# A two-layer graph attention kernel on one core: rows loaded one unit ahead, softmax work moved, bias rows prepared in pass one

## The chip, the core and the metric

The kernel runs on one core of a Trainium2 chip. Five engines work side by side: TensorE (PE; its weight loads are listed as PEld), VectorE (DVE), ScalarE (ACT), GpSimd (POOL) and SyncE (SP), which here issues every DMA. Each engine takes its instructions in the order of the program, and an instruction waits until what it reads has been written and what it overwrites has been read. Times are device microseconds (us); the metric is the time of one execution.

## What is computed

The input x has 128 batch entries of 64 rows by 768 columns, adj one 64 by 64 mask per entry. With `h = relu(layernorm(x))`, two layers follow:

```
m_left, m_right = h @ W_left.T, h @ W_right.T
u = h @ m_left.T / temper            (upper triangle and diagonal of adj)
  + h @ m_right.T / temper           (lower triangle)
e = exp(u) * adj
attention = e / (sum(e, axis=2) + 1e-10)
ctx = attention @ (h @ W_lin.T + b_lin)
h = relu(layernorm(ctx) * ln_a + ln_b)
```

The result is x plus the h of the second layer. Everything is float32.

## The kernel before, in words

The batch is cut into 16 units of 512 rows (T = 512, NB = 16). Each layer makes two passes over the units. **Pass one** projects a unit with W_left (k = 0) and W_right (k = 1) and makes its attention; **pass two** makes h @ W_lin, the context and the layer norm. In layer 0 pass two leaves its rows in DRAM, and pass one of layer 1 reads them back.

`project(u, k, g)` (lines 291 to 325) makes a third of one projection as seven groups of matmuls (a Strassen-like scheme, table ORDER at line 121). A unit has 42 such groups. Four PSUM banks, X, Y, Z and V, each with one buffer, take the groups in the order X Y Z V X Z V. ACT empties X (lines 312 and 320), DVE empties Y, Z and V (lines 315, 318, 322), and a bank is written again two or three groups later. So PE stops soon after DVE or ACT stops. The sums of token halves, T1 to T4 (line 140), are made on POOL; group Y reads T2, the first Z reads T1, the first V T3 and the last V T4. `scores(u)` (line 327) runs on PE between the second and third group of unit u + 1.

All other work of a pass is cut into steps that wait in a list, `queue`. After each group `pump(1)` (line 325) puts one step into the program; `flush()` puts all that are left. Where a step stands in the list thus sets where its instructions stand on every engine. For the next unit the steps are, in the order of the list before:

- the softmax chain of the unit just scored, in six steps (lines 341 to 365), with its eight stores of `att`;
- in layer 0, the statistics and the scaling of the new rows (lines 211 to 228); then four block transposes (line 257) and `store`, four DMAs to DRAM (line 250);
- `load_h` (line 191), which reads the transposed unit back as `ht`, four empty steps, and in layer 1 six `affine` steps, ScalarE's scaling and relu of `ht` (line 198);
- the four sums T1 to T4 and the masks `wm` (line 281).

The DMAs that load the rows and the masks `adj` of unit u + 1 are issued by `load` (line 269) in unit u after its first project, behind the stores of `att`. In the second unit (u = 1) of each pass one, `one_aside` also loads W_lin, centres it (`centre`, line 96) and makes its sums on POOL. Pass two begins with the load of the bias rows b1 and b2 and the arithmetic on them (lines 420 to 428). In the last unit of pass two of layer 0, rows of layer 1's first unit are loaded, transposed and scaled (lines 560 and 561).

Of the kernel before, what the change touches and what calls it, by code (L numbers as in the profile page):

```python
# [10 lines left out]
F32 = mybir.dt.float32  # L11
I32 = mybir.dt.int32
AF = mybir.ActivationFunctionType
# [4 lines left out]
def kernel(  # L18
# [60 lines left out]
    def flush(keep=0):  # L79
        pump(len(queue) - keep)  # L80
# [99 lines left out]
    def load_rows(l, u, pool):  # L180

        XR[l, u] = []
        for g in range(2):
            t = pool.tile([P, 2, H], F32, name="x", bufs=2)
            for a in range(4):
                i = 4 * g + a
                src = x[u * NBB + i] if l == 0 else ROWS[u][i]
                nc.sync.dma_start(t[a * 32:(a + 1) * 32], src.rearrange("(k j) h -> j k h", k=2))
            XR[l, u].extend([t[:, 0, :], t[:, 1, :]])

    def load_h(which, l, u):
        ht = HT[which, l, u] = big.tile([P, C, T], F32, name="ht")
        nc.sync.dma_start(ht, KEPT[l][u])

    def affine(which, l, u):

        for c in range(C if l else 0):
            queue.append(lambda c=c: nc.scalar.activation(  # L198
                HT[which, l, u][:, c, :], HT[which, l, u][:, c, :], AF.Relu,
                bias=b_col[:, c:c + 1], scale=a_col[:, c:c + 1]))  # L200

    def transpose_rows(l, u, pool):

# [41 lines left out]
            queue.append(lambda: nc.sync.dma_start(KEPT[l][u], ht))  # L245
            return

        xb = pool.tile([P, H // 32, Q, 32], F32, name="n" if pool is big else "xb", bufs=2 if pool is big else 1)

        def store():  # L250
            to = KEPT[l][u].rearrange("(b i) c t -> i c b t", b=4)
# [5 lines left out]
            queue.append(lambda q=q: nc.vector.transpose(  # L257
                xb[:, :, q, :], xr[q].rearrange("p (b j) -> p b j", j=32)))
        queue.append(store)
        queue.append(lambda: load_h(1, l, u))  # L260
        queue.extend([lambda: None] * 4)
        affine(1, l, u)


    def pass_one(l, aside):
        with tc.tile_pool(name=f"one{l}", bufs=2, reuse_waits="tile") as sp:
            ADJ, WM = {}, {}

            def load(u):
                if (l, u) not in XR:  # L270
                    load_rows(l, u, sp)
# [55 lines left out]
            def scores(u):  # L327
# [36 lines left out]
                        for g in range(2):  # L364
                            nc.sync.dma_start(to[a // 2, a % 2, g], at[a * 32:(a + 1) * 32, g])  # L365

                it = chain()
                for _ in range(6):
                    queue.append(lambda: next(it, None))

            for u in range(NB):
                if u == 0:
                    load(0)
                    if l == 0:
                        load_w(0, "l")
                        prepare(0, nc.vector)

                        flush(keep=5)
                        tokens = [queue.popleft() for _ in range(5)]
                        sums_w(0, "l", nc.vector)  # L380
                        sums = [queue.popleft() for _ in range(4)]
                        queue.extend(sums[:2] + tokens[:2] + [sums[2], tokens[2], sums[3], tokens[3], tokens[4]])
                        load_w(0, "r")
                        sums_w(0, "r", nc.gpsimd)
                    else:
                        prepare(0)
                    flush()
                    load(1)
                for g in range(CH):
                    project(u, 0, g, (lambda: scores(u - 1)) if u and g == 0 else None)  # L390
                    if g == 0:
                        if u and u + 1 < NB:
                            load(u + 1)
                        if u + 1 < NB:
                            prepare(u + 1)
                        else:
                            load_h(2, l, 0)
                            queue.extend([lambda: None] * 4)
                            affine(2, l, 0)
                            sums_t((2, l, 0))  # L400
                        if u in aside:
                            aside[u]()
                for g in range(CH):
                    project(u, 1, g)
                flush()
            scores(NB - 1)
            flush()


    def pass_two(l, aside):  # L410
        last = l == L - 1
        with tc.tile_pool(name=f"two{l}", bufs=2, reuse_waits="tile") as sp:
            rows = {}

            def row(name, src, n0=0, n1=H):
                t = sp.tile([P, n1 - n0], F32, name=name, bufs=1)
                nc.sync.dma_start(t, bass.AP(tensor=src.tensor, offset=src.offset + n0, ap=[[0, P], [1, n1 - n0]]))
                rows[name] = t

            row("b1", b_lin[l], 0, HH)  # L420
            row("b2", b_lin[l], HH, H)
            bm = stat.tile([P, 2], F32, name="bm", bufs=1)
            nc.vector.reduce_sum(bm[:, 0:1], rows["b1"], axis=mybir.AxisListType.X)
            nc.vector.reduce_sum(bm[:, 1:2], rows["b2"], axis=mybir.AxisListType.X)
            nc.vector.tensor_add(bm[:, 0:1], bm[:, 0:1], bm[:, 1:2])
            nc.vector.tensor_scalar_mul(bm[:, 0:1], bm[:, 0:1], -1.0 / H)
            nc.gpsimd.tensor_sub(rows["b2"], rows["b2"], rows["b1"])
            nc.vector.tensor_scalar_add(rows["b1"], rows["b1"], bm[:, 0:1])
            if last:
                row("a", ln_a[l])  # L430
                row("b", ln_b[l])
            AT, HL = {}, {}

            def load(u):
# [21 lines left out]

            def finish(u, r):
                cx = context(u, r)
                zs = [sp.tile([P, H], F32, name="z", bufs=2 if last else 4) for _ in range(2)]
                xs = []  # L460
                if last:
                    for k in range(2):
# [83 lines left out]
            for u in range(NB):  # L546
                for r in range(2):
                    before = None
                    if u or r:
                        before = lambda: finish(*((u, 0) if r else (u - 1, 1)))  # L550
                    kept = list(queue)
                    queue.clear()
                    beside = deque()
                    nxt = (2, l, u + 1) if u + 1 < NB else None if last else (1, 1, 0)
                    if r == 0:
                        if u + 1 < NB:
                            load(u + 1)
                            affine(*nxt)
# [3 lines left out]
                        if u + 1 < NB:  # L562
                            queue.extendleft([lambda: None] * (7 - len(queue)))
                        if u in aside:
                            loaded = aside[u]()
                    else:
                        if nxt:
                            sums_t(nxt)
# [57 lines left out]
```

## Time and profile before

| | |
|---|---|
| median of three runs | 3449.06 us (3445.66 to 3449.86) |
| profiled execution, its own time | 3446.99 us |
| its span, first to last instruction | 3445.2 us |
| PE busy | 3020.3 us, 88% of the span |
| POOL / DVE / ACT busy | 770.7 / 1142.9 / 586.5 us |
| mean granted TensorE clock | 0.937 of full speed |

The busy times are totals over passes with different limits. The granted clock is either 1.0 or 0.5 in a stretch (2.4 or 1.2 GHz), so a mean below 1 tells what share of the time it stood at the lower level. Of a wait the profile gives the engine that waited, the instruction that ended the wait, and the line of each.

### The profile page before, as it was taken

What the parts mean: (1) busy time and instruction counts of PE and PEld (TensorE: products, weight loads), DVE (VectorE), ACT (ScalarE), POOL (GpSimd) and SP (SyncE); (2) the same over time, 40 slices, a digit from 0 to 9 for tenths busy, and PEclk for the clock granted to TensorE, in tenths of its full rate; (3) what the DMA queues carried; (4) which work ended last, traced back from release to release, by engine and by line L of the source; (5) the groups of instructions that cost most, each with busy time, mean ns of one, the idle gap of its engine ahead of it and who ended that gap; (6) DMA issues with size and microseconds to landing.
All of it is one profiled execution on the core that took longest, in us unless ns stands there. A gap on an engine that the chain in (4) does not pass through costs nothing. (4 is left out here: it accounts for less than half of the span.)

```text
span 3445.2 us, 37340 instructions
## 1 busy us (share of the span) xinstructions
PE 3020.3 (88%) x14872; PEld 2310.3 (67%) x14872; DVE 1142.9 (33%) x2310; ACT 586.5 (17%) x1114; POOL 770.7 (22%) x484
## 2 busy tenths in 40 slices
PE   7888888888888899999787888877887789999998
PEld 6777777777777655555576777766776678555554
DVE  4433333333333232223232222222222222466555
ACT  2111111111111122222211111111111111222221
POOL 2210011000110253232103100000000111455554
PEclk9998999989999999999898999998898889999999
DMA  5323322223222243333432222223232220455554
GB/s 153 88 71 72 78 79 60 73 70 78 78 60 78 72 148 103 106 115 113 116 88 60 60 60 60 61 63 77 64 74 70 71 60 21 141 159 147 165 165 125
DMA packets 228718, 310.22 MB, mean 90 GB/s; under 512 B 53696, under 2 KB 179136, under 8 KB 220352
## 3 DMA queue, kind: packets, MB, share of 16 engines
q1 hardware_dynamic: 228544, 307.84, 32.8%
q8 instruction: 117, 1.92, 0.2%
q14 instruction: 57, 0.47, 0.0%
HBM read 202.91 MB, written 104.86 MB: 89 GB/s over the span
## 5 line engine op out<-in xcount | busy, mean ns | idle before, releaser
L140 POOL TENSOR_TENSOR ts<-ht 128x768 f32<-128x768 f32 x126 | 243.5, 1933 | 2069.6 <-ACT ht L198 850.3
L301 PE MATMUL Z<-ht,w_l_S 128*128 128x256 f32 x576 | 182.6, 464 | 250.5 <-DVE u L318 250.5
L301 PE MATMUL X<-ht,w_r_A 128*128 128x256 f32 x1152 | 302.0, 401 | 111.8 <-ACT n L320 111.8
L301 PEld LDWEIGHTS X<-ht,w_r_A 128*128 128x128 f32 x1152 | 229.5, 201 | 150.6 <-ACT n L320 117.8
L301 PEld LDWEIGHTS Z<-ht,w_l_S 128*128 128x128 f32 x576 | 130.0, 232 | 283.0 <-DVE u L318 262.1
L301 PE MATMUL V<-ts,w_l_A 128*128 128x256 f32 x1152 | 306.0, 406 | 0.3 <-DVE n L322 0.3
L516 PE MATMUL X<-w_n_A,ht 128*128 128x384 f32 x768 | 273.0, 492 | 17.7 <-DVE s L521 17.7
L301 PE MATMUL X<-ht,w_l_A 128*128 128x256 f32 x1152 | 281.0, 380 | 2.5 <-ACT s L312 2.5
L301 PE MATMUL V<-ts,w_r_A 128*128 128x256 f32 x1152 | 280.0, 379 | 0.0
L516 PE MATMUL V<-w_n_A,ts 128*128 128x384 f32 x768 | 268.8, 486 | 0.0
L301 PEld LDWEIGHTS V<-ts,w_l_A 128*128 128x128 f32 x1152 | 239.7, 208 | 40.5 <-DVE n L322 1.7
L315 DVE TENSOR_TENSOR u<-Y,s 128x256 f32<-128x256 f32 x192 | 80.3, 418 | 507.8 <-PE Y L301 454.8
L322 DVE TENSOR_TENSOR n<-V,u 128x256 f32<-128x256 f32 x384 | 161.6, 421 | 255.4 <-PE V L301 251.5
L140 POOL TENSOR_TENSOR ts<-ht,ts 128x768 f32<-128x768 f32 x126 | 238.8, 1895 | 26.4 <-issue 24.5
L301 PEld LDWEIGHTS X<-ht,w_l_A 128*128 128x128 f32 x1152 | 220.7, 192 | 34.8 <-ACT s L312 3.3
L301 PEld LDWEIGHTS V<-ts,w_r_A 128*128 128x128 f32 x1152 | 218.9, 190 | 29.8
L516 PEld LDWEIGHTS X<-w_n_A,ht 128*128 128x128 f32 x768 | 147.2, 192 | 121.4 <-DVE s L521 19.0
L516 PEld LDWEIGHTS V<-w_n_A,ts 128*128 128x128 f32 x768 | 146.2, 190 | 102.2 <-issue 0.8
L472 ACT ACTIVATE z<-aux 128x768 f32<-128x768 f32 x128 | 102.5, 806 | 622.5 <-PE aux L450 622.4
L198 ACT ACTIVATE ht<-ht,b_col,a_col 128x512 f32<-128x512 f32 x192 | 142.2, 804 | 328.0 <-DMA ht<-h 328.0
L312 ACT COPY s<-X 128x256 f32<-128x256 f32 x192 | 71.4, 372 | 738.9 <-PE X L301 732.8
L320 ACT COPY n<-X 128x256 f32<-128x256 f32 x192 | 71.1, 370 | 701.0 <-PE X L301 700.8
(102 smaller groups left out, 3864.0 us busy)
## 6 DMA issues: line engine op xcount, KB each, us to landing
ht<-h SPq DMA_DIRECT2D x63, 1536.0 KB, 6.5
h<-xb SPq DMA_DIRECT2D x120, 384.0 KB, 6.0
x<-in_x_dram SPq DMA_DIRECT2D x128, 192.0 KB, 4.8
z<-z SPq DMA_DIRECT2D x128, 192.0 KB, 2.9
x<-z SPq DMA_DIRECT2D x128, 192.0 KB, 4.7
xr<-in_x_dram SPq DMA_DIRECT2D x128, 192.0 KB, 4.0
out_dram<-xr SPq DMA_DIRECT2D x128, 192.0 KB, 2.7
adj<-in_adj_dram SPq DMA_DIRECT2D x64, 128.0 KB, 6.0
```

What stands on the lines that cost most here:

```text
L140: eng.tensor_sub(b[o], b[m], b[n])
L198: queue.append(lambda c=c: nc.scalar.activation(HT[which, l, u][:, c, :], HT[which, l, u][:, c, :], AF.Relu, bias=b_col[:, c:c + 1], scale ...
L301: nc.tensor.matmul(p, w[a][:, c, g * P:(g + 1) * P], b[t][:, c, :], start=(new and c == 0), stop=(c == CH - 1), skip_group_check=True)
L312: nc.scalar.copy(s1, p)
L315: nc.vector.tensor_add(u2, p, s1)
L320: nc.scalar.copy(to, pb)
L322: nc.vector.tensor_add(to, pb, (u4 if i == 3 else u2).rearrange("p (b s) -> p b s", s=S))
L472: nc.scalar.activation(zs[k].rearrange(two, n=2), cx[k], AF.Square, accum_out=ss[:, k:k + 1])
L516: nc.tensor.matmul(p, b[t][:, c, r * P:(r + 1) * P], w[a][:, c, :], start=(new and c == 0), stop=(c == CH - 1), skip_group_check=True)
```

## The change

- `load_rows` for unit u + 2 is now a step of unit u, behind `load_h` of unit u + 1; before, the rows of unit u + 1 were loaded in unit u. The steps of a unit begin with the first project, not with the second, so the statistics or transposes come first.
- The six softmax steps stand behind `load_h` and `load_rows`; then come `load_adj`, six empty steps, the six affine steps in layer 1, masks, T1 and T2. T3 and T4 (`late`) are put in during the last project of the unit.
- In the last unit the next pass's `load_h` and its affine steps and sums take these places.
- The bias rows are loaded, and worked on as one more step, in unit 1 of pass one (`bias`, called from `one_aside`).
- At the end of pass two of layer 0, layer 1's first rows are loaded in unit 14, transposed in its second half, and read back and scaled in unit 15. Affine steps of pass two go in pairs, those of layer 1's first unit in threes; z has two buffers where it had four in layer 0.

The core of the diff (the new `affine` with a step, and `row`, moved out of pass two, are left out):

```diff
@@ transpose_rows
         queue.append(store)
-        queue.append(lambda: load_h(1, l, u))
-        queue.extend([lambda: None] * 4)
-        affine(1, l, u)
@@ pass_one
-            def prepare(u, eng=nc.gpsimd):
-                if (1, l, u) not in TS:
-                    transpose_rows(l, u, sp)
-                    sums_t((1, l, u), eng)
-                queue.append(lambda: masks(u))
+            def softmax(u):
+                return [lambda: next(CHAIN[u], None)] * 6
+            def prepare(u):
+                transpose_rows(l, u, sp)
+                queue.append(lambda: load_h(1, l, u))
+                if u + 1 < NB:
+                    queue.append(lambda: load_rows(l, u + 1, sp))
+                queue.extend(softmax(u - 2) if u > 1 else [lambda: None] * 6)
+                queue.append(lambda: load_adj(u))
+                queue.extend([lambda: None] * 6)
+                affine(1, l, u)
+                queue.append(lambda: masks(u))
+                sums_t((1, l, u))
...
-                it = chain()
-                for _ in range(6):
-                    queue.append(lambda: next(it, None))
+                CHAIN[u] = chain()
...
+            load_rows(l, 1, sp)
             for u in range(NB):
                 if u == 0:
+                    queue.extend([lambda: None] * 7)
+                if u + 1 < NB:
+                    prepare(u + 1)
+                else:
+                    queue.extend([lambda: None] * 6)
+                    queue.append(lambda: load_h(2, l, 0))
+                    queue.extend(softmax(u - 1) + [lambda: None] * 4)
+                    affine(2, l, 0)
+                    sums_t((2, l, 0))
+                late = [queue.pop() for _ in range(2)][::-1]
+                for k in range(2):
+                    for g in range(CH):
+                        project(u, k, g, (lambda: scores(u - 1)) if u and k == g == 0 else None)
+                        if k == g == 0 and u in aside:
                             aside[u]()
-                for g in range(CH):
-                    project(u, 1, g)
+                        if k == 1 and g == CH - 2:
+                            flush()
+                            queue.extend([lambda: None] * 3 + late)
                 flush()
...
+    def bias(l):
+        row("b1", b_lin[l], 0, HH, big)
+        row("b2", b_lin[l], HH, H, big)
+        b1, b2 = rows["b1"], rows["b2"]
+        bm = stat.tile([P, 2], F32, name="bm", bufs=1)
+        def centred():
+            nc.vector.reduce_sum(bm[:, 0:1], b1, axis=mybir.AxisListType.X)
+            nc.vector.reduce_sum(bm[:, 1:2], b2, axis=mybir.AxisListType.X)
+            nc.vector.tensor_add(bm[:, 0:1], bm[:, 0:1], bm[:, 1:2])
+            nc.vector.tensor_scalar_mul(bm[:, 0:1], bm[:, 0:1], -1.0 / H)
+            nc.gpsimd.tensor_sub(b2, b2, b1)
+            nc.vector.tensor_scalar_add(b1, b1, bm[:, 0:1])
+        queue.append(centred)
@@ pass_two
-                        elif nxt:
-                            load_rows(1, 0, sp)
-                            transpose_rows(1, 0, big)
+                            if turn:
+                                load_rows(1, 0, sp)
+                        elif turn:
+                            queue.append(lambda: load_h(1, 1, 0))
+                            queue.extend(nop * 4)
+                            affine(1, 1, 0, 3)
@@ one_aside
             load_w(l, "n")
+            bias(l)
             centre(l)
```

On PE the order of the work is unchanged. Three places show the new order.

The SP queue in a steady unit of layer 0's pass one (`h_8` is the transposed unit 8, `att_6` the attention of unit 6, `x` rows), before:

```order
L365 DMA att_6_131<-at 128x1x32 x8
L188 DMA x<-in_x_dram 32x2x768 x8
L274 DMA adj<-in_adj_dram 64x4x128 x2
L253 DMA h_8_85<-xb 192x4x128 x4
L193 DMA ht<-h_8_85 128x3072
```

and now:

```order
L256 DMA h_8_85<-xb 192x4x128 x4
L193 DMA ht<-h_8_85 128x3072
L188 DMA x<-in_x_dram 32x2x768 x8
L373 DMA att_6_131<-at 128x1x32 x8
L272 DMA adj<-in_adj_dram 64x4x128 x2
```

The rows x were those that the four stores of h_8 wait for; now they are those of unit 9. The masks `adj` came ahead of the store and are now the last of the turn.

DVE where the statistics of new rows begin in layer 0 (Y, Z and V rows empty banks, the first of them in the unit's second group), before:

```order
L355 RECIPROCAL s<-s 128x4
L356 TENSOR_TENSOR v<-v,s 128x256
L322 TENSOR_TENSOR n<-V,u_961 128x4x64
L360 STREAM_TRANSPOSE at<-v 128x4x2x32
L174 BN_STATS st<-x 128x6 x2
L175 BN_AGGR mv_1071<-st 128x2
L315 TENSOR_TENSOR u_1090<-Y,s_1080 128x256
L174 BN_STATS st<-x 128x6 x2
L175 BN_AGGR mv_1071<-st 128x2
L318 TENSOR_TENSOR u_1100<-Z,u_1090 128x256
```

and now:

```order
L330 TENSOR_TENSOR n<-V,u_943 128x4x64
L174 BN_STATS st<-x 128x6 x2
L175 BN_AGGR mv_972<-st 128x2
L323 TENSOR_TENSOR u_991<-Y,s_981 128x256
L174 BN_STATS st<-x 128x6 x2
L175 BN_AGGR mv_972<-st 128x2
L326 TENSOR_TENSOR u_1052<-Z,u_991 128x256
```

The statistics follow the last V of the unit before; the softmax rows stand behind the transposes.

POOL in unit 1 of layer 0 (`ts` are T1 to T4, `wm` the masks, `w_n` is W_lin, `b` the bias rows), before:

```order
L140 TENSOR_TENSOR ts<-ht 128x768
L140 TENSOR_TENSOR ts<-ht,ts 128x768
L140 TENSOR_TENSOR ts<-ht 128x768
L140 TENSOR_TENSOR ts<-ht,ts 128x768
L281 TENSOR_TENSOR wm<-adj,tri 128x4x64 x2
L110 TENSOR_TENSOR w_n_A_703<-w_n_A_703,wm 128x1152
```

and now:

```order
L279 TENSOR_TENSOR wm<-adj,tri 128x4x64 x2
L140 TENSOR_TENSOR ts<-ht 128x768
L140 TENSOR_TENSOR ts<-ht,ts 128x768
L439 TENSOR_TENSOR b_713<-b_713,b_711 128x384
L110 TENSOR_TENSOR w_n_A_700<-w_n_A_700,wm 128x1152
L110 TENSOR_TENSOR w_n_A_701<-w_n_A_701,wm 128x1152
L110 TENSOR_TENSOR w_n_A_703<-w_n_A_703,wm 128x1152
L110 TENSOR_TENSOR w_n_A_702<-w_n_A_702,wm 128x1152
L118 TENSOR_TENSOR w_n_S_704<-w_n_A_701,w_n_A_702 128x1152
L118 TENSOR_TENSOR w_n_S_705<-w_n_S_704,w_n_A_700 128x1152
L118 TENSOR_TENSOR w_n_A_701<-w_n_A_700,w_n_A_701 128x1152
L118 TENSOR_TENSOR w_n_S_706<-w_n_A_703,w_n_S_705 128x1152
```

The masks now precede the sums, and T3 and T4 of this unit (the next two L140 rows in the queue) stand behind all the work on W_lin; in every other unit they follow T2 directly.

## Rows read from the trace of the kernel before

**Rows 1.** Each pass: us; busy us (instructions) of PE, PEld, DVE, ACT, POOL; PEclk; DMA.

```profile
22.70:1158.30 1135.60, 1000.66 (x5570) 872.84 (x5568) 385.95 (x884) 177.23 (x313) 164.79 (x106) 0.93 0.29 75
1158.30:1668.20 509.90, 491.66 (x1858) 271.49 (x1856) 145.24 (x303) 119.97 (x225) 166.77 (x105) 0.98 0.38 118
1668.20:2930.30 1262.10, 1030.24 (x5572) 889.69 (x5569) 306.81 (x670) 150.19 (x311) 156.06 (x104) 0.90 0.26 65
2930.30:3445.20 514.90, 492.11 (x1858) 271.57 (x1856) 295.24 (x429) 130.41 (x252) 280.60 (x157) 0.98 0.53 151
```

**Rows 2.** What PE waited for, whole span: total us, times, longest.

```profile
PE Z L301 <- DVE u L318: 251.4, 30, 11.5
PE X L301 <- ACT n L320: 111.8, 15, 8.9
PE X L516 <- DVE s L521: 17.7, 2, 9.1
```

**Rows 3.** Timeline (start us, us, engine, line, xcount) of PE without a stall, end of layer 0's pass one.

```profile
1103.63 1.46 PE L301 MATMUL X<-ht,w_l_A 128*128 128x256 f32 x6
...
1152.94 5.46 PE L335 MATMUL aux<-n,ht 128*64 128x128 f32 x96
1158.33 2.20 PE L516 MATMUL X<-w_n_A,ht 128*128 128x384 f32 x6
```

**Rows 4.** Timeline of a stall in layer 0; [idle before, and what ended it].

```profile
397.29 3.82 SPq L188 DMA_DIRECT2D x<-in_x_dram  x8
...
403.30 1.02 DVE L174 BATCH_NORM_STATS2 st<-x 128x6 f32<-128x384 f32 x2 [11.20 <-DMA x<-in_x_dram]
...
406.43 2.93 PE L301 MATMUL Z<-ht,w_l_S 128*128 128x256 f32 x6 [8.66 <-DVE u L318]
...
409.16 2.61 PE L301 MATMUL V<-ts,w_l_A 128*128 128x256 f32 x6
...
420.91 5.21 SPq L253 DMA_DIRECT2D h<-xb  x4
```

**Rows 5.** Timeline of layer 1's second stall: store, load back, affine.

```profile
2253.95 5.21 SPq L253 DMA_DIRECT2D h<-xb  x4
...
2264.43 0.34 SPq L193 DMA_DIRECT2D ht<-h  x1
...
2271.35 0.81 ACT L198 ACTIVATE ht<-ht,b_col,a_col 128x512 f32<-128x512 f32 x1 [14.02 <-DMA ht<-h]
```

**Rows 6.** Timeline around the stalls of layer 0's pass two: first unit, last unit.

```profile
1174.35 0.42 DVE L428 TENSOR_SCALAR b<-b,bm 128x384 f32<-128x384 f32 x1 [1.07 <-POOL b L427]
...
1650.86 4.33 ACT L198 ACTIVATE ht<-ht,b_col,a_col 128x512 f32<-128x512 f32 x6 [19.17 <-DMA ht<-h]
...
1659.73 4.21 PE L516 MATMUL Z<-w_n_S,ht 128*128 128x384 f32 x6 [9.09 <-DVE u L529]
```

**Rows 7.** Groups by line: xcount | busy us, mean ns | idle before.

```profile
L140 POOL TENSOR_TENSOR ts<-ht 128x768 f32<-128x768 f32 x126 | 243.5, 1933 | 2069.6 <-ACT ht L198 850.3 <-DMA ht<-h 735.6 <-PE Y L301 292.8
L281 POOL TENSOR_TENSOR wm<-adj,tri 128x256 f32<-128x256 f32 x64 | 45.1, 726 | 24.9 <-DMA adj<-in_adj_dram 24.9
L110 POOL TENSOR_TENSOR w_n_A<-w_n_A,wm 128x1152 f32<-128x1152 f32 x8 | 16.6, 2114 | 0.0
L118 POOL TENSOR_TENSOR w_n_S<-w_n_A,w_n_A 128x1152 f32<-128x1152 f32 x2 | 5.3, 2626 | 0.2
L103 DVE TENSOR_REDUCE wm<-w_n_A 128x3 f32<-128x1152 f32 x4 | 5.4, 1341 | 0.0
```

**Rows 8.** DMA issues: KB each, median us from issue to landing.

```profile
ht<-h SPq DMA_DIRECT2D x63, 1536.0 KB, 6.5
x<-z SPq DMA_DIRECT2D x128, 192.0 KB, 4.7
w_n_A<-in_w_lin_dram SPq DMA_DIRECT2D x8, 576.0 KB, 7.7
adj<-in_adj_dram SPq DMA_DIRECT2D x64, 128.0 KB, 6.0
```

More of the change, by code (lines that the diff above doesn't have):

```diff
@@ L193, in load_h, with affine, part @@
         nc.sync.dma_start(ht, KEPT[l][u])
[L195 to L200, printed above, removed]
+    def affine(which, l, u, step=1):
+        def part(c0):
+            for c in range(c0, c0 + step):
+                ht = HT[which, l, u][:, c, :]
+                nc.scalar.activation(ht, ht, AF.Relu, bias=b_col[:, c:c + 1], scale=a_col[:, c:c + 1])
+        for c in range(0, C if l else 0, step):
+            queue.append(lambda c=c: part(c))
     def transpose_rows(l, u, pool):
@@ L246, in transpose_rows @@
             return
-        xb = pool.tile([P, H // 32, Q, 32], F32, name="n" if pool is big else "xb", bufs=2 if pool is big else 1)
+        xb = pool.tile([P, H // 32, Q, 32], F32, name="xb", bufs=1)
         def store():
@@ L259, in transpose_rows, with load_adj @@
         queue.append(store)
-        queue.append(lambda: load_h(1, l, u))
-        queue.extend([lambda: None] * 4)
-        affine(1, l, u)
     def pass_one(l, aside):
         with tc.tile_pool(name=f"one{l}", bufs=2, reuse_waits="tile") as sp:
[L267 to L271, printed above, removed]
+            ADJ, WM, CHAIN = {}, {}, {}
+            def load_adj(u):
                 ADJ[u] = sp.tile([P, Q, 2, S], F32, name="adj")
@@ L365, in chain @@
                             nc.sync.dma_start(to[a // 2, a % 2, g], at[a * 32:(a + 1) * 32, g])
-                it = chain()
-                for _ in range(6):
-                    queue.append(lambda: next(it, None))
+                CHAIN[u] = chain()
+            if (l, 0) not in XR:
+                load_rows(l, 0, sp)
+            load_adj(0)
+            if l == 0:
+                load_w(0, "l")
+                transpose_rows(0, 0, sp)
+                flush()
+                sums_t((1, 0, 0), nc.vector)
+                tokens = [queue.popleft() for _ in range(4)]
+                sums_w(0, "l", nc.vector)
+                sums = [queue.popleft() for _ in range(4)]
+                queue.extend(sums[:2] + tokens[:2] + [sums[2], tokens[2], sums[3], tokens[3]])
+                load_w(0, "r")
+                sums_w(0, "r", nc.gpsimd)
@@ L371, in pass_one @@
+            queue.append(lambda: masks(0))
+            flush()
+            load_rows(l, 1, sp)
             for u in range(NB):
                 if u == 0:
[L373 to L386, printed above, removed]
@@ L387, in pass_one @@
-                    flush()
-                    load(1)
-                for g in range(CH):
[L390 to L401, printed above, removed]
+                    queue.extend([lambda: None] * 7)
@@ L402, in pass_one, with row @@
                             aside[u]()
-                for g in range(CH):
-                    project(u, 1, g)
+                        if k == 1 and g == CH - 2:
+                            flush()
+                            queue.extend([lambda: None] * 3 + late)
                 flush()
             scores(NB - 1)
+            queue.extend(softmax(NB - 1))
             flush()
+    rows = {}
+    def row(name, src, n0, n1, pool):
+        t = rows[name] = pool.tile([P, n1 - n0], F32, name=name, bufs=1)
+        nc.sync.dma_start(t, bass.AP(tensor=src.tensor, offset=src.offset + n0, ap=[[0, P], [1, n1 - n0]]))
@@ L412, in pass_two @@
         with tc.tile_pool(name=f"two{l}", bufs=2, reuse_waits="tile") as sp:
[L413 to L428, printed above, removed]
             if last:
-                row("a", ln_a[l])
-                row("b", ln_b[l])
+                row("a", ln_a[l], 0, H, sp)
+                row("b", ln_b[l], 0, H, sp)
             AT, HL = {}, {}
@@ L458, in finish @@
                 cx = context(u, r)
-                zs = [sp.tile([P, H], F32, name="z", bufs=2 if last else 4) for _ in range(2)]
+                zs = [sp.tile([P, H], F32, name="z", bufs=2) for _ in range(2)]
                 xs = []
@@ L553, in pass_two @@
                     beside = deque()
-                    nxt = (2, l, u + 1) if u + 1 < NB else None if last else (1, 1, 0)
+                    nop = [lambda: None]
+                    turn = not last and u >= NB - 2
                     if r == 0:
@@ L557, in pass_two @@
                             load(u + 1)
-                            affine(*nxt)
-                        elif nxt:
-                            load_rows(1, 0, sp)
-                            transpose_rows(1, 0, big)
-                        if u + 1 < NB:
-                            queue.extendleft([lambda: None] * (7 - len(queue)))
+                            queue.extend(nop * 3)
+                            affine(2, l, u + 1, 2)
+                            if turn:
[4 more added lines that the diff above has]
+                            affine(1, 1, 0, 3)
+                        queue.extend(nop * (7 - len(queue)))
                         if u in aside:
@@ L566, in pass_two @@
                     else:
-                        if nxt:
-                            sums_t(nxt)
+                        if u + 1 < NB:
+                            sums_t((2, l, u + 1))
+                            if turn:
+                                transpose_rows(1, 0, sp)
+                        elif turn:
+                            sums_t((1, 1, 0))
                         if u in aside:
```

## The prediction
> **What bounds the kernel now.** Read the passes first [rows 1]. Both passes two are nearly full: PE is busy for 491.7 of 509.9 us and 492.1 of 514.9, at a granted clock of 0.98. The loss is in the passes one, 1135.6 and 1262.1 us for the same work, at 0.93 and 0.90. Next, what PE waits for [rows 2]: 30 waits end with DVE's line 318 (251.4 us), 15 with ACT's line 320 (111.8 us). Both lines only empty banks, in under half a microsecond; they are late because something ahead of them on their engine is. The timelines say what. In layer 0 DVE stands at the statistics of new rows until the rows land, 11.2 us, and PE behind it for 8.66 [rows 4]. In layer 1 DVE stands at the transposes in the same way, and a second time ACT stands 14.0 us at the first affine step, whose `ht` was asked for only 6.9 us earlier [rows 5].
>
> How long would a pass one be without stalls? In [rows 3] no row has idle time before it: from 1103.63 to 1152.94 are 38 groups, 1.298 us each, and the scores take 5.4 (to 1158.33). A unit is 42 x 1.298 + 5.4 = 59.9 us, sixteen are 958. Against [rows 1], stalls cost 1135.6 - 958 = 177 us in layer 0 and 1262.1 - 958 = 304 in layer 1. That is more than PE's idle time, since after a stall two groups run at the lower clock: 2.93 and 2.61 us where 1.46 is usual [rows 4], some 2.6 us per stall.
>
> **The change part by part.** I give places in a unit as us from its start; group n ends at 1.3 n, and 5.4 later from the third on.
>
> *Layer 0, statistics.* The rows of unit u + 2 are now issued in unit u behind `load_h`, some 35 us before they are used; one such set needs 397.29 to 403.30, 6 us, before DVE can start [rows 4]. The wait goes in all units but unit 0: there the seven empty steps keep the statistics where they stood, and its rows are loaded where they were. I leave one stall, 8.4 (251.4/30) + 2.6, about 10. Gain 177 - 10 = 167.
>
> *Layer 1.* The transposes gain in the same way. The affine steps: the store now comes at about 12 (two transposes must follow the banks emptied behind the scores). From store to the first affine took 17.4 us (2253.95 to 2271.35) [rows 5], so `ht` is there at 29.4. The first affine stands behind group 21, at 5.4 + 27.3 = 32.7; PE would stop only if the X of group 22 were not copied by the second X, at 37.9. The cover is 3 us to ACT and about 7 to PE. It would shrink if the rows, 8 x 192 KB issued just behind `ht`, shared its transfer: at most doubled, 6.5 us more [rows 8], which uses up that cover and no more. Gain 304.
>
> *Bias, turn of the layers.* The stalls at the start of both passes two (17.7 us together [rows 2]) and in the last unit of layer 0's pass two (9.09, behind six affine steps in one piece [rows 6]) have their cause moved away. With some 2.4 us each of slow groups (4.21 where 2.10 is usual [rows 6]) that is 27 + 7 = 34.
>
> *What becomes late next: the masks.* In layer 0, statistics to store took 403.30 to 420.91, 17.6 us [rows 4]; begun at 0.5, with the scores between, the store comes at 23.5. `load_h` waits 10.5 for its landing [rows 5] (34), lands 7 later (41), the rows behind it need another 7 (48), the eight `att` stores about 1.5, then `adj` 3 to 6 [rows 8]: 53 to 55.5. POOL then makes two halves of the masks (1.45) and T1 and T2 (1.93 each [rows 7]), done at 58.3 to 60.8. The next unit's second group needs T2 at 61.2. T3 and T4 follow by 64.7, needed from 69.2. I take no stall, with 0.4 to 3 us of cover. The softmax steps (DVE, ACT) fall where nothing waits; their `att` stores are inside this turn.
>
> *Unit 1 with W_lin.* Here the added work is not free. DVE's update of b1 must wait for POOL's subtraction, which reads b1 and stands behind masks, T1 and T2. In layer 0 DVE gets there at about 49 and POOL at 58 + 1.0: ten microseconds in which no bank is emptied. Then come two rounds of reductions (2 x 1.34 and small ones each [rows 7]). PE loses about 12 with its slow groups. POOL's four subtractions (2.1 each) and four sums (2.6 each [rows 7]) now stand ahead of T3 and T4, 19 us; T3 comes some 3 us late, 6 with slow groups: 18 in all. In layer 1 the weights are issued behind the rows (4 x 576 KB, about 11 us at the rate of `ht`), `adj` behind them, so POOL is as late, and DVE reaches b1 at 46: 13 us of block, 15 lost, 1 more for T3: 16. For the two units I take 34, with ends 0 (POOL early, DVE never blocked) and 60 (the block twice as long).
>
> *Small ends:* where passes change, memory taken over from the last `att` stores, and ACT between affine and squares: 4, ends 0 and 10.
>
> **Sum.** 167 + 304 + 34 - 34 - 4 = 467. From the span of 3445.2 that leaves 2978; this execution's own time lies 1.8 us above its span, so **2980 us**. The execution's 3446.99 stands 2 us below the median of the runs, 3449.06, within their scatter. About 0.2%, 7 us, is what a measurement of this kernel tells from no change.
>
> **Rivals.**
>
> *Late masks.* The turn of SP grows by a few us more, and PE waits at each unit's second group in layer 0 (line 140 ends the wait). Against: 0.4 to 3 us of cover with each transfer set behind the last. For: that cover is thin, and 8 small stores are between. A miss of 2 to 5 us in 14 units is 28 to 70: 3008 to 3050. Chance 0.12.
>
> *Late `ht` in layer 1.* If rows and `ht` share the transfer and the rest slips too, ACT stands at the affine as now. One stall of 111.8/15 = 7.5 [rows 2] + 2.6 in 14 units is 141: about 3121. Against: the 7 us of cover. Chance 0.05.
>
> *The clock does not come back.* PE's waits sum to some 394 us (380.9 in [rows 2] and 13 in single ones), the stalls to about 515 (177 + 304 + 34): 121 us are slow groups. If short waits for banks kept the clock dropping even so, about 110 of them stay: 3090. Against: both passes two hold 0.98 with the same four banks [rows 1], and the groups of [rows 3] are all at full speed. The Trainium skill ("TensorE: Matmul & The Clock Gate", A second HAM failure mode: psum-queue depth-cycling) states that cycling through PSUM banks can make PE idle so often and briefly that its clock swings between the levels; by that page this rival would be the forecast, and no stretch here without a long stall shows it. Chance 0.04.
>
> *The early load does nothing.* If the rows are still behind in SP's queue when DVE asks, layer 0 keeps its 167 and the forecast is 3147. Against: the 35 us. Chance 0.02.
>
> *Slower: SP's turn longer than a unit.* A unit now takes 75 us on average, (1135.6 + 1262.1)/32 [rows 1]. Everything of the next unit hangs on `adj` at the end of SP's turn. If each of its 23 DMAs waited for the landing of the last, the turn would be about 23 x 4 to 6 us behind the store at 23.5, 115 and more: 40 us over today's unit, some 28 x 40 = 1100 above 3447, about 4500. It decides from the point where `adj` lands beyond 70, 15 later than worked out. Against: today's eight row loads are issued in 3.82 us, none waiting for another [rows 4]. Chance 0.02.
>
> **How the numbers follow.** The forecast has 0.75. Its own range: 34 can be 0 to 60, the small ends 0 to 10, unit 0's stall 6 to 11, which gives 2940 to 3012; all ends at zero together is unlikely, so I start at 2950. Taking in late masks up to 3050 leaves out the other rivals, 0.13, and the edges. Range 2950 to 3050. Faster by over 0.2%: 0.97, all cases but the last, less 0.01 for a mixture of several that ends within 0.2%; slower: 0.02.
>
> **What would show it.** The list of PE's waits should lose nearly all of lines 318 and 320 (in the old numbering): from 45 to some 5. Pass one should take about 980 us in both layers, at a granted clock near 1.0. What remains should stand in units 0 and 1 of layer 0 and in unit 1 of layer 1, ended by DVE behind the bias update (waiting for POOL), and by POOL's T3 in unit 2. Waits ended by line 140 at the second group of every unit of layer 0 would show late masks; waits of X on ACT in layer 1 a late `ht`; full busy at a clock below 0.97 the clock. A pass one above 1020 us in either layer makes the forecast wrong.

## The result and the profile after

| | before | after |
|---|---|---|
| median | 3449.46 us (4 runs, 3445.66 to 3450.26) | 2994.46 us (4 runs, 2993.47 to 2995.75) |
| ratio | | 0.8683, 95% interval 0.8668 to 0.8698 |
| span of the profiled execution | 3445.2 us | 2994.0 us |
| PE busy | 3020.3 us, 88% | 2919.1 us, 97% |
| mean granted clock | 0.937 | 0.992 |

Forecast: 2980 us, 2950 to 3050, faster. The time lies 14 us above the forecast and inside the range.

The passes of the kernel after, in the columns of [rows 1]:

```profile
21.80:1011.70 989.90, 968.46 (x5570) 852.30 (x5569) 381.51 (x889) 173.54 (x312) 166.58 (x109) 0.99 0.33 87
1011.70:1503.60 491.90, 489.01 (x1859) 270.38 (x1857) 143.10 (x298) 120.18 (x226) 165.86 (x104) 1.00 0.39 122
1503.60:2477.70 974.10, 962.60 (x5569) 848.85 (x5568) 307.75 (x675) 150.79 (x311) 156.75 (x105) 0.99 0.33 85
2477.70:2994.00 516.30, 493.81 (x1858) 272.15 (x1856) 294.31 (x424) 130.30 (x252) 279.60 (x156) 0.99 0.53 150
```

The passes one lost 145.7 and 288.0 us, the first pass two 18.0. The last pass two, 514.9 before, is no shorter. DVE, ACT and POOL did the same work as before; only its place changed.

What PE waits for, in the columns of [rows 2]. Line 326 was line 318, 328 was 320, 535 was 516, and 548 was 529:

```profile
PE Z L309 <- DVE u L326: 17.5, 4, 8.9
PE aux L240 <- DMA adj<-in_adj_dram: 12.2, 1, 12.2
PE Z L535 <- DVE u L548: 7.9, 2, 5.0
PE Z L309 <- DVE n L330: 6.9, 1, 6.9
...
PE V L309 <- POOL ts L140: 3.7, 2, 3.4
PE Y L309 <- POOL ts L140: 2.6, 1, 2.6
```

The 30 waits on line 318 are 4, the 15 on ACT's line 320 are gone, and so are the two at the bias rows (17.7 us). The 12.2 us are the start of the kernel.

A steady unit of layer 0, in the columns of [rows 3, 4]:

```profile
346.46 1.46 PE L309 MATMUL X<-ht,w_l_A 128*128 128x256 f32 x6
...
370.42 5.48 SPq L256 DMA_DIRECT2D h<-xb  x4
381.00 0.35 SPq L193 DMA_DIRECT2D ht<-h  x1
381.44 6.91 SPq L188 DMA_DIRECT2D x<-in_x_dram  x8
389.05 6.62 SPq L373 DMA_DIRECT2D att<-at  x8
395.71 1.30 SPq L272 DMA_DIRECT2D adj<-in_adj_dram  x2
399.39 1.41 POOL L279 TENSOR_TENSOR wm<-adj,tri 128x256 f32<-128x256 f32 x2 [51.17 <-DMA adj<-in_adj_dram]
...
402.65 1.81 POOL L140 TENSOR_TENSOR ts<-ht,ts 128x768 f32<-128x768 f32 x1
...
407.73 1.46 PE L309 MATMUL Y<-ts,w_l_S 128*128 128x256 f32 x6
```

The unit begins at 346.46 with its first X. The store is issued 24.0 us later, `load_h` 34.5, the masks' load 49.3, and T2 is done at 402.65 + 1.81 = 404.46, or 58.0. The next unit's Y, which reads T2, starts at 407.73 without a wait: 3.3 us of cover. In the steady units nothing on DVE waits for rows any more. From one start of the scores to the next lie 60.0 us in each of the units 3 to 14, in both layers (forecast: 59.9).

### The profile page after: what moved, and what is told of

It is laid out like the page before. It is cut to its first block, busy times and chain, and to the rows that moved or that the text cites. A ratio compares the mean times of both kernels' runs of the same rounds, so it can differ in the third digit from the quotient of the medians.

```text
span 2994.0 us, 37473 instructions
## 1 busy us (share of the span) xinstructions
PE 2919.1 (97%) x14872; PEld 2248.1 (75%) x14872; DVE 1135.8 (38%) x2310; ACT 583.2 (19%) x1112; POOL 769.9 (26%) x484
## 4 chain that ended last, share of the span: by engine, by line
PE 89%; DMA 4%; POOL 2%; DVE 2%; SPq 1%; ACT 1%; issue 1%; DVEq 0%; POOLq 0%; ACTq 0%
PE Z L309 15%; PE V L309 15%; PE X L309 15%; PE Z L535 8%; PE Y L309 8%; PE V L535 7%; PE X L535 7%; PE aux L343 5%; PE Y L535 4%; PE aux L469 3%; DMA x<-in_x_dram 1%; DMA xr<-in_x_dram 1%; POOL ts L140 1%; DMA h<-xb 1%; POOL w_n_S L118 1%
## 5 line engine op out<-in xcount | busy, mean ns | idle before, releaser
L279 POOL TENSOR_TENSOR wm<-adj,tri 128x256 f32<-128x256 f32 x64 | 45.1, 726 | 1393.9 <-DMA adj<-in_adj_dram 1306.0
L140 POOL TENSOR_TENSOR ts<-ht 128x768 f32<-128x768 f32 x126 | 243.7, 1934 | 289.4 <-PE Y L309 156.1
L309 PE MATMUL V<-ts,w_l_A 128*128 128x256 f32 x1152 | 282.0, 381 | 4.3 <-POOL ts L140 3.7
L309 PE MATMUL X<-ht,w_r_A 128*128 128x256 f32 x1152 | 280.0, 379 | 0.0
L309 PEld LDWEIGHTS V<-ts,w_l_A 128*128 128x128 f32 x1152 | 219.8, 191 | 35.6 <-POOL ts L140 4.5
L309 PEld LDWEIGHTS X<-ht,w_r_A 128*128 128x128 f32 x1152 | 218.9, 190 | 29.8
L140 POOL TENSOR_TENSOR ts<-ht,ts 128x768 f32<-128x768 f32 x126 | 239.0, 1897 | 4.6 <-issue 2.1
L330 DVE TENSOR_TENSOR n<-Z,u 128x256 f32<-128x256 f32 x192 | 81.3, 424 | 305.0 <-PE Z L309 304.9
L326 DVE TENSOR_TENSOR u<-Z,u 128x256 f32<-128x256 f32 x192 | 81.4, 424 | 284.2 <-PE Z L309 283.8
L545 POOL TENSOR_TENSOR u2b<-u,b 128x384 f32<-128x384 f32 x64 | 63.8, 997 | 476.6 <-DVE u L543 463.1
```

Of the source, the lines that this page charges most:

```text
L309: nc.tensor.matmul(p, w[a][:, c, g * P:(g + 1) * P], b[t][:, c, :], start=(new and c == 0), stop=(c == CH - 1), skip_group_check=True)
L326: nc.vector.tensor_add(u4, p, u2)
L330: nc.vector.tensor_add(to, pb, (u4 if i == 3 else u2).rearrange("p (b s) -> p b s", s=S))
L545: nc.gpsimd.tensor_add(u2b, u2, rows["b2"])
```

## The experiments

Pass lengths, from the first matmul of a pass to the first of the next, in the profiled executions; medians beside them:

| | pass one, layer 0 | pass two | pass one, layer 1 | pass two | median us |
|---|---|---|---|---|---|
| before | 1135.6 | 509.9 | 1262.1 | 514.9 | 3449.5 |
| after | 989.9 | 491.9 | 974.1 | 516.3 | 2994.5 |
| e1: before, rows early | 969.9 | 511.0 | 1136.4 | 518.3 | 3156.9 |
| e2: after, softmax in front | 1041.3 | 490.4 | 1113.8 | 512.1 | 3180.2 |
| e3: after, no empty steps | 991.4 | 493.2 | 1001.1 | 512.1 | 3015.2 |
| e4: after, bias in pass two | 984.8 | 504.0 | 966.1 | 513.5 | 2995.6 |
| e5: after, b2 - b1 on DVE | 984.3 | 493.3 | 967.8 | 509.6 | 2982.4 |
| e6: after, adj ahead of rows | 977.4 | 493.3 | 965.5 | 510.6 | 2970.5 |
| e7: after, stalls taken out | 965.7 | 487.3 | 962.3 | 503.6 | 2943.6 |
| e8: e7 and e6 | 960.7 | 487.2 | 962.0 | 503.5 | 2937.8 |

### e1: the early rows alone

In the kernel before, the rows of unit u + 1 are issued at the head of unit u, ahead of the stores of `att`, and nothing else moves. They are still loaded in the unit that uses them.

```diff
-            def load(u):
-                if (l, u) not in XR:
+            def load(u, rows=True):
+                if rows and (l, u) not in XR:
...
+                if u and u + 1 < NB:
+                    load_rows(l, u + 1, sp)
...
-                            load(u + 1)
+                            load(u + 1, False)
```

> The kernel before with one thing moved: the eight row loads of unit u + 1 are issued ahead of unit u's scores and its eight attention stores; they still stand in the unit before their use, and every compute step stays where it was. Theory (the place in SP's queue is what counts, not the distance in units): SP no longer stands at the attention stores before it can issue the rows, so all layer 0 stalls but unit 0's go and the first of layer 1's two; layer 1's second (X on ACT, about 6 to 7.5 us and 2.6 of slow groups, 15 times) and the stalls of pass two stay: about 3140 us. Rival (the rows must be asked for a unit ahead): DVE still waits for the rows, above 3400 us.

Measured: 3156.88 us, ratio 0.916 (0.9142 to 0.9179), near the theory's 3140. PE's waits in e1 (line 301 as in [rows 2]):

```profile
PE X L301 <- ACT n L320: 132.2, 15, 12.6
...
PE Z L301 <- DVE u L318: 5.8, 2, 5.5
```

Of the 30 waits behind DVE 2 are left, those behind ACT stay, and the units of layer 0 last 60.0 us, one 61.4. So what made the rows late was their place on SP's queue: behind eight stores that wait for the softmax of the same unit. A unit's lead was not needed for that. The rows alone take 165.7 us from layer 0, where the forecast's term was 167, and 125.7 from layer 1.

### e2: the softmax steps back in front

```diff
+                queue.extend([lambda: None])
+                queue.extend(softmax(u - 2) if u > 1 else [lambda: None] * 6)
                 transpose_rows(l, u, sp)
                 queue.append(lambda: load_h(1, l, u))
                 if u + 1 < NB:
                     queue.append(lambda: load_rows(l, u + 1, sp))
-                queue.extend(softmax(u - 2) if u > 1 else [lambda: None] * 6)
                 queue.append(lambda: load_adj(u))
-                queue.extend([lambda: None] * 6)
+                queue.extend([lambda: None] * 2)
                 affine(1, l, u)
```

> The changed kernel with its six softmax steps back at the front of a unit's list (one empty step ahead of them), and between the load back and the first affine step only the row loads, the masks' load and two empty steps; rows are still one unit ahead. Theory (the steps between store, load back and affine are the cover): in layer 1 X waits on ACT again, 6 us and 2.6 of slow groups in each of 14 units; in layer 0 the store comes some 9 us later, so the masks and T2 miss the second group by 3 to 6 us in 14 units: 3130 to 3230 us, pass one of layer 1 about 1095. Rival (the rows a unit ahead are all that mattered): within 10 us of 2994.

Measured: 3180.2 us, ratio 0.9228 (0.921 to 0.9247), inside the theory's range. PE's waits:

```profile
PE X L310 <- ACT n L329: 115.9, 15, 12.0
PE Y L310 <- POOL ts L140: 40.9, 13, 11.8
```

The stall on ACT is back in layer 1: the distance between store and affine is what had removed it, and pass one of layer 1 is 139.7 us longer than after the whole change. Counted in steps of the list, the first affine stands 5 behind `load_h` in the kernel before and in e2, and 15 behind it in the kernel after. The second line is the rival of late masks, now real: twelve waits of 1.8 to 3.4 us in steady units of layer 0 (3 to 6 were expected) and one of 11.8 at the start of unit 1. A unit of layer 0 in e2:

```profile
344.47 9.05 SPq L188 DMA_DIRECT2D x<-in_x_dram  x8
...
353.95 1.57 SPq L272 DMA_DIRECT2D adj<-in_adj_dram  x2
...
360.20 1.41 POOL L279 TENSOR_TENSOR wm<-adj,tri 128x256 f32<-128x256 f32 x2 [56.67 <-DMA adj<-in_adj_dram]
...
363.45 1.80 POOL L140 TENSOR_TENSOR ts<-ht,ts 128x768 f32<-128x768 f32 x1
...
365.30 2.93 PE L310 MATMUL Y<-ts,w_l_S 128*128 128x256 f32 x6 [3.38 <-POOL ts L140]
```

T2 is done at 365.25, and the Y group that reads it starts at 365.30 after 3.38 us of waiting. With 3.3 us of cover in the kernel after, seven steps in front of the transposes were enough to use it up. Pass one of layer 0 is 1041.3 - 989.9 = 51.4 us longer, 42.3 of it in the units 3 to 14.

### e3: without the six empty steps

```diff
                 queue.append(lambda: load_adj(u))
-                queue.extend([lambda: None] * 6)
                 affine(1, l, u)
```

> The changed kernel without the six empty steps ahead of the affine steps; the softmax steps stay between load back and affine. Theory (the cover of the affine steps is 7 us to PE): ACT reaches the first affine 7.8 us earlier, stands there until ht lands about 30 us into the unit, and runs four affine steps before it empties X, about 1 us late: 0 to 1.5 us in each of 14 units of layer 1, no slow groups, 2994 to 3015 us, X waits on ACT in the list of waits. Rival (the empty steps carry the gain): the old stall of 7.5 us comes back, about 3130.

Measured: 3015.16 us, ratio 0.8747 (0.8733 to 0.8762), just above the theory's range; the profiled execution was the slowest of four, 7.3 us above the median. In a steady unit of layer 1 ACT now waits 4.5 us for `ht`, and PE waits for ACT ten times:

```profile
PE V L308 <- DVE n L329: 31.0, 4, 15.3
...
PE X L308 <- ACT n L327: 11.5, 10, 3.1
```

The 31.0 us were not expected. With six steps fewer in the list, the bias step in unit 1 comes earlier; in layer 1 DVE waits there 6.87 us for the bias rows to land and then 9.60 for POOL, and PE 15.3 where it waited 8.9. Unit 1 grew by 6.2 us. So of the 27 us that the empty steps are worth in layer 1, only a part is the distance from store to affine. With 9 steps from `load_h` to the first affine, PE's waits for ACT are 11.5 us; with 5 (e2) they are 115.9. So the distance comes mostly from the softmax steps.

### e4: the bias rows back at the start of pass two

```diff
         with tc.tile_pool(name=f"two{l}", bufs=2, reuse_waits="tile") as sp:
+            bias(l)
+            flush()
...
             load_w(l, "n")
-            bias(l)
             centre(l)
```

> The changed kernel with the bias rows loaded and worked on at the start of pass two, as before. Theory (the bias step costs in unit 1 about what it saves): DVE's wait for POOL in unit 1 of both layers goes (6.95 + 1.85 and 8.85 us and slow groups, some 23 in all); the stalls at the start of both passes two come back (9.15 and 8.57 and slow groups), but the one of layer 1 hides the 5.00 us stall that now follows it there: 2980 to 2992 us. Rival (the bias step is worth the 22 us that it removed): 3010 to 3020.

Measured: 2995.63 us, ratio 0.8691 (0.8678 to 0.8704): the same time as after, neither theory's. By passes: the wait at the start of the passes two is back (17.7 us in two waits), which costs 12.1 us in layer 0 and nothing that shows in layer 1 (2.8 shorter than after, 1.4 to 3.9 longer than in e2, e3, e5 and e6); and the passes one are 5.1 and 8.0 shorter without the bias in unit 1. Moving the bias rows took about as much in unit 1 as it gave at the turn.

### e5: the difference of the bias rows on VectorE

```diff
-            nc.gpsimd.tensor_sub(b2, b2, b1)
+            nc.vector.tensor_sub(b2, b2, b1)
```

> The changed kernel, with the difference of the two bias rows (b2 - b1) taken on VectorE instead of GpSimd. The theory: in unit 1 of each pass one VectorE's update of b1 stands 10 us (layer 0: 10.85, layer 1: 9.89) for GpSimd's subtraction, which is queued behind the masks and the first two token sums, and TensorE waits for VectorE's evictions behind it (6.95 + 1.85 us and 8.85 us), with half-clock stretches of 6.8 and 10.2 us after it. Without that wait: 15 to 23 us off, 2972 to 2980 us. Rival: unit 1 is long because of the other work for W_lin there (GpSimd's 25 us of subtractions and sums ahead of the third token block); then the time stays within 5 us of 2994.

Why unit 1 of layer 0 is long in the kernel after:

```profile
143.40 1.40 POOL L279 TENSOR_TENSOR wm<-adj,tri 128x256 f32<-128x256 f32 x2 [50.75 <-DMA adj<-in_adj_dram]
...
148.40 0.99 POOL L439 TENSOR_TENSOR b<-b,b 128x384 f32<-128x384 f32 x1
149.42 0.42 DVE L440 TENSOR_SCALAR b<-b,bm 128x384 f32<-128x384 f32 x1 [10.85 <-POOL b L439]
...
150.23 2.93 PE L309 MATMUL Z<-ts,w_r_S 128*128 128x256 f32 x6 [6.95 <-DVE n L330]
```

DVE stands 10.85 us for a subtraction of 0.99, which is queued on POOL behind masks that wait for their load. Measured: 2982.36 us, ratio 0.8649 (0.8637 to 0.8661), 12 us off, less than the theory's 15 to 23 and more than the rival's 5. The wait is gone, and another has grown in its place:

```profile
PE V L309 <- POOL ts L140: 9.7, 2, 9.0
```

PE now comes to unit 2's T3 earlier, and T3 still stands behind the work on W_lin; 3.39 us of wait became 9.02, and in e4, which has no bias step in unit 1, 9.54. Both were true: the block hid part of what POOL's work costs. Of the 16.4 us between the two profiled spans, 6.7 are pass two of layer 1, which the edit does not touch. That pass lasted 509.6 to 512.1 us in e2, e3, e5 and e6 and 516.3 in the kernel after, though its work is the same in all; where these us lie is told below, under "Bias and turn".

### e6: the masks ahead of the rows

```diff
-                if u + 1 < NB:
-                    queue.append(lambda: load_rows(l, u + 1, sp))
                 queue.extend(softmax(u - 2) if u > 1 else [lambda: None] * 6)
                 queue.append(lambda: load_adj(u))
+                if u + 1 < NB:
+                    queue.append(lambda: load_rows(l, u + 1, sp))
```

> The changed kernel, with the load of the next unit's rows put back behind the stores of the attention block and the load of the masks, still one unit ahead of its use. Theory: what mattered was that rows no longer arrive behind stores that wait for the same unit's softmax; with a unit of lead they may stand behind the stores, since these leave 381 to 396 us into a stretch whose rows are wanted at 407: 2985 to 2998 us, and the masks, now ahead of the rows on SyncE's queue, arrive some 4 to 8 us earlier. Rival: any place behind the stores is late; then the next unit's statistics wait on VectorE again in the 14 steady units of layer 0 and the time is above 3050 us.

Measured: 2970.48 us, ratio 0.8615 (0.8603 to 0.8627), better than the theory, and the rival's late statistics did not come. Its steady unit of layer 0, which begins at 334.69:

```profile
369.61 6.59 SPq L373 DMA_DIRECT2D att<-at  x8
376.25 1.30 SPq L272 DMA_DIRECT2D adj<-in_adj_dram  x2
377.64 4.03 SPq L188 DMA_DIRECT2D x<-in_x_dram  x8
```

The masks' load is issued 41.6 us into the unit, where it was 49.3, and no steady unit waits for the rows: all last 60.0 us. So a place behind the stores is late only without the unit of lead. Most of the gain, which the expectation did not count, is in the units 1: everything POOL does there waits for the masks, so DVE's wait for b2 - b1 in layer 0 shrinks from 10.85 to 2.67 us, and T2 of unit 1 is no longer late (2.61 before this edit). Some 6 us are again pass two of layer 1.

### e7 and e8: a version without the remaining stalls

e7 takes the remaining waits one by one. With `spare`, a list filled in unit 2, the W_lin work goes ahead of the masks, where POOL stands idle:

```diff
-            nc.gpsimd.tensor_sub(b2, b2, b1)
+            nc.vector.tensor_sub(b2, b2, b1)
@@ prepare
                 queue.append(lambda: load_adj(u))
-                queue.extend([lambda: None] * 6)
+                queue.extend([lambda: None, lambda: None, lambda: spare and spare.popleft()()] * 2)
@@ pass_one, unit 0
             load_rows(l, 1, sp)
+            if l == 0:
+                load_w(0, "r")
+                sums_w(0, "r", nc.gpsimd)
...
             scores(NB - 1)
+            load_h(2, l, 1)
@@ pass_two
             load(0)
+            if last:
+                row("a", ln_a[l], 0, H, sp)
+                row("b", ln_b[l], 0, H, sp)
...
                         elif turn:
+                            affine(1, 1, 0, 3)
                             sums_t((1, 1, 0))
```

> The changed kernel with its remaining stalls taken one by one: b2 - b1 on VectorE; the subtractions and sums for W_lin one or two steps a unit from unit 2 on, ahead of the masks, where GpSimd stands some 50 us a unit waiting for them; the rows of unit 1 ahead of W_right on SyncE's queue; the second block of pass two loaded right behind the last scores, and ln_a and ln_b behind the first attention block; the two affine steps of layer 1's first block half a unit later, when the block has arrived. Theory (each remaining wait is what it seems): some 25 us in pass one of layer 0 (units 1 and 2 lasted 71.9 and 65.3 us against 60.0, and 8 us of unit 0), 12 in that of layer 1 (71.4 and 60.6), 5 and 8 in the two passes two: 2935 to 2960 us. Rival: GpSimd's pieces collide with VectorE's work wherever they are put, and units 2 to 8 grow by 1 to 3 us each: 2960 to 2980 us.

Measured: 2943.55 us, ratio 0.8539 (0.8527 to 0.8551), as the theory has it. The longest wait left after the start is this one:

```profile
PE Y L311 <- POOL ts L142: 3.0, 1, 3.0
```

Putting e6's order on top:

> The kernel of e7_spread with the masks' load ahead of the next unit's rows on SyncE's queue, as in e6_rows_behind. Theory: of the waits of e7_spread one of 3.05 us is left in layer 0, in unit 1, where the second token sum waits for GpSimd, and GpSimd for the masks, which land at 77 us behind the rows; with it goes a half-clock stretch of 3.4 us: 4 to 5 us off, 2937 to 2941 us, and one unbroken stretch of full clock. Rival: TensorE is the bound everywhere and what one place gives another takes: 2942 to 2946 us.

Measured: 2937.79 us, ratio 0.8522 (0.8511 to 0.8534), as the theory has it and 56.7 us below the kernel after. From just before the first projection of e8 (22.61) to 4.8 us behind the end of its last matmul (2922.08), in the columns of [rows 1]:

```profile
22.30:2926.90 2904.60, 2896.99 (x14853) 2236.26 (x14851) 1122.73 (x2286) 573.18 (x1100) 763.75 (x469) 1.00 0.38 105
```

PE is busy for 99.7% of it at full clock. What could still be gained without fewer matmuls is the first 22 us, the 13.9 us behind the last matmul, and 2.8 us of waits between.

## Why the prediction was right, point by point

**The chains.** Both were as forecast. Rows behind stores that wait for the softmax: shown by e1. Store, load back and affine too close together: shown by e2, where it returns with the softmax steps in front. The sum by passes, against the profiled spans:

| term | forecast | measured |
|---|---|---|
| layer 0, pass one: 167 - 18 for unit 1 | -149 | -145.7 |
| layer 1, pass one: 304 - 16 for unit 1 | -288 | -288.0 |
| bias and turn, layer 0's pass two | -23 | -18.0 |
| bias, layer 1's pass two | -11 | +1.4 (-2.8 to -5.3 in e2, e3, e5, e6) |
| small ends | +4 | -1 (ahead of the first projection; the rest lies in the passes) |
| span | -467 | -451 |

The first two terms are close, and in part by luck. In layer 0 the one stall left, in unit 0, was written as 8.4 + 2.6, "about 10", which adds to 11; its wait measured 5.42. In layer 1 unit 1 cost 12.0 where 16 was written, and the rest came out 4 us longer than 16 x 59.9, as in e8, whose pass of 962.0 has hardly a wait.

**Bias and turn: the step that failed.** The 34 us of "27 + 7 = 34" measured 16.6: 18.0 in layer 0 less 1.4 in layer 1 (a gain of 3 to 5 there, by the four kernels that ran the same pass in 509.6 to 512.1 us; 11 in none of them). The cause of the first stall was moved away, and in layer 1 the next one, which it had hidden, took its place. What becomes late next was asked for the masks and not here. In the kernel after:

```profile
2487.80 0.53 SPq L425 DMA_DIRECT2D a<-in_ln_a_dram  x1
...
2489.45 0.33 SPq L193 DMA_DIRECT2D ht<-h  x1
...
2498.82 4.33 ACT L200 ACTIVATE ht<-ht,b_col,a_col 128x512 f32<-128x512 f32 x6 [19.30 <-DMA ht<-h]
...
2506.37 0.17 DVE L494 TENSOR_SCALAR rs<-sd 128x2 f32<-128x2 f32 x1 [12.30 <-ACT sd L493]
...
2508.97 3.26 PE L535 MATMUL Z<-w_n_S,ht 128*128 128x384 f32 x5 [5.00 <-DVE u L548]
```

The block `ht` is asked for at 2489.45, behind the last stores of `att` and three loads. ACT stands 19.30 us at its affine steps, DVE 12.30 behind ACT's square root, PE 5.00 behind DVE. In e4 the bias wait of 8.48 us comes before it, and there is no such wait on Z. In layer 0's last unit the same form remains at 2.89 us (9.09 before [rows 6]). e7, which asks for the block earlier and, at the turn of the layers, moves the affine steps, took 4.6 and 12.7 us from the two passes two.

Of the 12.7, some 4 are something else, and so are most of the 4 to 7 by which e2, e3, e5 and e6 are shorter there. They lie at two places of the kernel after, at 2687.53 and 2719.92; the first is:

```profile
2681.83 4.34 ACT L200 ACTIVATE ht<-ht,b_col,a_col 128x512 f32<-128x512 f32 x6 [8.02 <-DMA ht<-h]
...
2683.55 0.96 DVE L504 SCALAR_TENSOR_TENSOR xr<-z,xr 128x768 f32<-128x768 f32 x1 [3.27 <-DMA xr<-in_x_dram]
...
2687.53 1.51 PE L469 MATMUL aux<-n,at 64*64 64x384 f32 x14 [1.24 <-DVE n L556]
```

The block `ht`, asked for at 2670.48, landed 11.3 us later, and the one at the second place 11.5; the other blocks of this pass took 8.4 to 9.4, and in e5 none took over 9.1. The rows of x behind them came late, DVE stood, and PE lost about 2 us each time against e5. The order of issue is that of e5, so these us are not of the change. Why two blocks landed late is open; in e1, whose pass is the longest (518.3), four took 10.5 to 12.1, and in the kernel before two took 10.4 and 11.8.

**Unit 1.** Forecast 18 and 16 us. Units 1 and 2 lasted 71.9 and 65.3 us in layer 0, 17.2 over twice 60.0, and 71.4 and 60.6 in layer 1, 12.0. The blocks were 10.85 and 9.89 us where 10 and 13 were written, and T3 was 3.39 us late where 3 was. In layer 1 POOL was earlier than worked out. What the text took as a fixed price was not one: it is the lateness of the masks, as e6 shows, and POOL has time in other units, as e7 shows.

**The masks.** Store at 24.0 (forecast 23.5), `load_h` at 34.5 (34), T2 at 58.0 (58.3 to 60.8), needed at 61.3 (61.2). At these points the chain was right to within a microsecond, in between by luck: from `load_h` to the first store of `att` 14 us were written and 8.0 measured (381.00 to 389.05), for the stores 1.5 and 6.7 (to 395.71). The two errors cancel. The cover was real but thin, as e2 shows.

**Late `ht` in layer 1.** The first affine of a steady unit ran without a wait, at 30.7 us into the unit:

```profile
1812.48 1.46 PE L309 MATMUL X<-ht,w_l_A 128*128 128x256 f32 x6
...
1835.40 0.34 SPq L193 DMA_DIRECT2D ht<-h  x1
...
1843.15 0.81 ACT L200 ACTIVATE ht<-ht,b_col,a_col 128x512 f32<-128x512 f32 x1
```

By the median of 7.4 us to landing, `ht` was there at 1842.8, 0.4 us earlier. The rows behind it made it 0.9 us slower (6.5 before [rows 8]), not twice as slow.

**The clock.** The rival fell. From 178.1 to 1495.4 us the granted clock of the kernel after was 1.0 throughout, with the same four banks in turn, and in e8 for 2904.6 us. So what the Trainium skill ("TensorE: Matmul & The Clock Gate", A second HAM failure mode: psum-queue depth-cycling) tells of another kernel does not show in this one: bank after bank alone did not lower the clock here. Between the first projection and the last matmul of the kernel after it fell to 0.5 at or right behind seven waits of TensorE (2.61, 2.89, 3.39, 5.00, 5.42, 6.95 and 8.85 us) and stayed at 1.0 through those of 1.85, 1.42, 1.24 and 1.16 us. The length of one wait alone does not decide: in e2 it fell 1.3 us behind one of 1.93 us and held through one of 3.10.

**Early load does nothing, SP's turn.** Neither came. The turn ends 49.3 + 1.3 us into a unit of 60.

## What to carry to other kernels

Where one queue issues all transfers, a load's delay is its place in that queue: look for stores ahead of it that wait for something late, and put what another engine waits for ahead of what has slack. Where a stall is taken away, follow each engine on to its next wait in the same stretch and price that too; here about half of what the term for bias and turn missed was a wait that a longer one had hidden. Extra work on a shared engine costs what stands behind it, so put it where that engine is idle, not where it was issued first.

## What the runs showed that was not expected

- Loads queued behind a large one wait for it, and the large one hardly notices: the rows' median landing went from 4.7 [rows 8] to 8.6 us, that of `ht` from 6.5 to 7.4. In e6, with the rows behind the masks, they are 4.9 and 6.6.

```profile
ht<-h SPq DMA_DIRECT2D x63, 1536.0 KB, 7.4
...
x<-z SPq DMA_DIRECT2D x128, 192.0 KB, 8.6
```

- A VectorE sum of 128 x 3 elements, 0.16 us alone, took 1.39 while GpSimd's subtractions for W_lin were running; the second of them ends at 157.34, the sum at 157.36:

```profile
152.73 0.16 DVE L105 TENSOR_TENSOR wm<-wm 128x3 f32<-128x3 f32 x1
...
153.17 4.17 POOL L110 TENSOR_TENSOR w_n_A<-w_n_A,wm 128x1152 f32<-128x1152 f32 x2 [3.78 <-DVE wm L106]
...
155.97 1.39 DVE L105 TENSOR_TENSOR wm<-wm 128x3 f32<-128x3 f32 x1
```

  The Trainium skill ("SBUF — State Buffer", Terms) says that the two engines share a port pair and that one blocks for a whole instruction of the other; these rows agree with it.
- Moving eight loads of rows behind the stores of `att` and two loads of masks was worth 24 us by the medians (e6; 5.7 of the 24.6 between the profiled spans are pass two of layer 1, which it does not touch); the move of the bias rows was worth about nothing (e4, 1.2 us).
